# Attention scores in four PSUM banks: one exponential of 2048 columns a round, or two of 1024

## The chip, the cores and the metric

The kernel runs on one core of one Trainium2 chip. The core has a matrix engine (PE, with its weight loads shown apart as PEld), a vector engine (DVE), an activation engine (ACT), a general-purpose engine (POOL) and a queue that issues transfers (SP). Each works through its own queue in order and waits on semaphores for the others. The matrix engine writes its results to PSUM, which this kernel uses as eight banks, each 512 float32 wide on 128 partitions; everything else here lives in SBUF or in main memory. The metric is the time of one execution on the device, in microseconds (us); the median of several is taken.

## The reference

The program is two layers of a transformer-like network on an input of 8 images, 128 channels and 32 x 32 = 1024 tokens, float32 throughout. The change touches only the first mixing step, an attention with 8 heads of 16 channels. Of the reference, what matters is this:

```python
q = (xp @ wq.T).reshape(b, h, w, n, d)
k = (xp @ wk.T).reshape(b, h, w, n, d)
v = (xp @ wv.T).reshape(b, h, w, n, d)
weights = jnp.einsum('bhwnd,bxynd->bnhwxy', q, k) * scale
weights = jax.nn.softmax(weights, axis=-1)
attn = jnp.einsum('bnhwxy,bxynd->bhwnd', weights, v)
```

The softmax runs over `y`, the 32 columns of one key row, and not over all 1024 keys: every query has 32 softmaxes for each head, one for each key row, and the results of all rows are added up. After the attention come a spectral convolution over the tokens, a convolution with learned offsets and a mixture of experts; they are not touched.

## The kernel before, in words

**Stages.** A first stage of some 28 us loads the weights and checks a bound on the scores, by which the kernel chooses `attention_bounded` (line 500). This attention runs over all 8 images. After it comes the spectral stage, mixed with the second layer, to the end of the program.

**Tiling of the attention.** An image has two head groups (`HG` = 2) of four heads (`NH` = 4), and four blocks of 256 queries (`QU` = 256). One head group of one query block is a *unit*: 8 units for an image, 64 in all. A unit takes four *rounds*, `r` = 0 to 3, one for each pair of key tiles of 128 keys; there are 256 rounds. In a round, `scores` (line 601) takes a tile `s` of 128 x 4 x 2 x 256 float32: head `j` has PSUM bank `j`, and within a bank the first 256 columns are key tile `c` = 0 and the second 256 are key tile `c` = 1. Eight matmuls fill it. In the program each float32 matmul is two instructions, so the profile counts 16. Then one activation takes the exponential of all 2048 columns into `e` in SBUF. The pool of `s` has one buffer (line 520), so the next round's matmuls wait until this exponential has read the banks.

**What follows a round's exponential.** `add_tiles` (line 620) adds the two key tiles on POOL. `sums` (line 626) contracts the sums over key columns on PE, all four `r` of a unit together, 32 instructions. `reciprocals` (line 635) inverts them on DVE, `spread_out` (line 639) spreads the result over the partitions on PE (tile `rb`, two banks), `divide` (line 649) multiplies `e` by it on DVE, `values` (line 655) multiplies with the values on PE, 16 instructions for an `r`. `take` and `results` hand a query block on. The projections of the next image (`keys`, `queries`, `key_values`, lines 560 to 599) and its normalisation are strewn between, each with a matmul group on PE and a copy on ACT. PSUM is full: four banks for `s`, two for `rb`, one for `av`, and one (`small_bank`, line 532) that `z` and all the small steps take in turn.

**What sets the order.** No planner: each step is entered in a list by `at(round, order, step)` (line 693), the list is sorted by round and then by order, and the steps are issued so (lines 758 to 760); every engine's queue has its instructions in this order. In a round, the order is `scores` (0), `add_tiles` (1), `values` (2), `spread_out` (2.5), `divide` (3), `sums` (4), `reciprocals` and `take` (5), pieces of other work (5.5, 6), and a half step of `values` (6.5). For a unit that starts in round `t0`, the sums come in `t0+5`, the spreading in `t0+6`, the divisions in `t0+6` to `t0+9`, the values in `t0+8` to `t0+11`. So the rounds have four kinds, by their number modulo four, and in the steady state PE's queue holds in each:

| kind | round mod 4 | PE's queue, in order |
|---|---|---|
| A | 0 | scores, values (16), pieces, values (8) |
| B | 1 | scores, values (8), sums (32) |
| C | 2 | scores, values (16), spread_out (8) |
| D | 3 | scores, values (16), pieces |

Of the kernel before, what the change touches and what calls it, by code (L numbers as in the profile page):

```python
# [11 lines left out]
F32 = mybir.dt.float32  # L12
I32 = mybir.dt.int32
AF = mybir.ActivationFunctionType
# [4 lines left out]
P = 128  # L19
# [6 lines left out]
HD = C // HEADS  # L26
# [37 lines left out]
def layer_norm_pieces(nc, pool, src, dst, eps):  # L64

    t = {}

    def stats(i):  # L70
        if i == 0:
            for name, shape in (
                ("st", [P, NT, 6]), ("mv", [P, NT, 2]), ("v", [P, NT]), ("y", [P, NT]),
                ("w", [P, NT]), ("nm", [P, NT]),
            ):
                t[name] = pool.tile(shape, F32, tag=f"lp_{name}", name=f"lp_{name}")
        nc.vector.bn_stats(t["st"][:, i, :], src()[:, i, :])
        nc.vector.bn_aggr(t["mv"][:, i, :], t["st"][:, i, :])

    def inverse(n):  # L80

        v, y, w, mv = t["v"], t["y"], t["w"], t["mv"]
        bits = [i.bitcast(I32) for i in (y, v)]
        ops = [
            lambda: nc.gpsimd.tensor_scalar(v, mv[:, :, 1], eps, None, ALU.add),
            lambda: nc.gpsimd.tensor_scalar(bits[0], bits[1], -0.5, 0x5F3759DF, ALU.mult, ALU.add),
            lambda: nc.gpsimd.tensor_scalar(v, v, -0.5, None, ALU.mult),
        ]
        ops += 3 * [
            lambda: nc.gpsimd.tensor_mul(w, y, y),  # L90
            lambda: nc.gpsimd.tensor_mul(w, w, v),
            lambda: nc.gpsimd.tensor_scalar(w, w, 1.5, None, ALU.add),
            lambda: nc.gpsimd.tensor_mul(y, y, w),
        ]
        ops += [
            lambda: nc.gpsimd.tensor_mul(t["nm"], mv[:, :, 0], y),
            lambda: nc.gpsimd.tensor_scalar(t["nm"], t["nm"], -1.0, None, ALU.mult),
        ]
        for op in ops[2 * n : 2 * n + 2]:
            op()  # L100

    def norm(i):
        nc.scalar.activation(
            dst()[:, i, :], src()[:, i, :], AF.Identity, bias=t["nm"][:, i : i + 1],
            scale=t["y"][:, i : i + 1],
        )

    return (
        [partial(stats, i) for i in range(NT)] + [partial(inverse, n) for n in range(9)]
        + [partial(norm, i) for i in range(NT)]  # L110
    )
# [288 lines left out]
class BoundedAttention:  # L400
# [3 lines left out]
    NH = 4  # L404
# [95 lines left out]
def attention_bounded(ctx, tc, ident, x, x1d, given, weigh, begin_group):  # L500
# [8 lines left out]
    nc = tc.nc  # L509
    NH, HG = given.NH, given.HG  # L510
    QU = 256
# [7 lines left out]
    ep = ctx.enter_context(tc.tile_pool(name="a_e", bufs=11))  # L519
    sp = ctx.enter_context(tc.tile_pool(name="a_s", bufs=1, space=PSUM))  # L520
    rp = ctx.enter_context(tc.tile_pool(name="a_r", bufs=1, space=PSUM))

    VB = 2 * (P + HD)
# [72 lines left out]
            pv.rearrange("p (a j d) -> p a j d", j=NH, d=HD),  # L598
        )

    def scores(img, un, r):

        qc, hg = un["at"]
        s = sp.tile([P, NH, 2, QU], F32, tag="s", name="s")
        q = img["q"][:, hg].rearrange("p a t -> p (a t)")
        for c in range(2):
            for j in range(NH):
                rows = slice(32 * j, 32 * j + 32)
                nc.tensor.matmul(  # L609
                    s[:, j, c, :], img["k"][rows, hg, 2 * r + c, :],  # L610
                    q[rows, qc * QU : (qc + 1) * QU], start=True, stop=True,
                )
        e = ep.tile([P, NH, 2, QU], F32, tag="e", name="e")
        nc.scalar.activation(  # L614
            e.rearrange("p j c q -> p (j c q)"), s.rearrange("p j c q -> p (j c q)"), AF.Exp,
            scale=float(HD) ** -0.5,
        )
        un["e", r] = e

    def add_tiles(un, r):  # L620
        t = sb.tile([P, NH, QU], F32, tag="t", name="t", bufs=6)
# [71 lines left out]
    def at(round_no, order, do, *args):  # L693
        work.append((round_no, order, len(work), do, args))

    def spread_rounds(pieces, rounds):
        for piece, round_no in zip(pieces, rounds):
            at(round_no, 6, piece)

    for b in range(B):  # L700
        img = {}
        first = 4 * UNITS * b
        project = [
            (keys, img, 0, 0), (keys, img, 0, 1), (queries, img, 0, 0),
            (keys, img, 1, 0), (keys, img, 1, 1), (queries, img, 1, 0),
            (key_values, b, img, 0), (key_values, b, img, 1),
            (queries, img, 0, 1), (queries, img, 1, 1),
        ]
        if b == 0:
            turn = {"tokens": (0, 0)}  # L710
            project_at = (-1, -1, -1, 0, 1, 2, 3, 4, 7, 11)
        else:
            project_at = [first + n for n in (-13, -12, -9, -5, -4, -1, 3, 4, 7, 11)]
            turn = {"channels": (first - 20, first - 17)}
            if b == 1:
                turn.update(load=0, tokens=(2, 3))
                norm_at = (3, 3, 4, 4, 5, 5, 6, 6) + (6, 7, 7, 8, 8, 8, 9, 9, 9) + (
                    10, 10, 10, 11, 13, 13, 14, 14)
            else:
                turn.update(load=first - 42, tokens=(first - 38, first - 34))  # L720
                norm_at = [first - n for n in (
                    37, 36, 35, 34, 33, 32, 32, 31, *range(31, 22, -1), 22, 22, 22, 21, 19, 19, 18, 18
                )]
        if b:
            at(turn["load"], 6, load, b)
            spread_rounds(
                layer_norm_pieces(nc, sb, lambda i=img: i["xt"], lambda: given.ht, 1e-6), norm_at
            )
            for par in range(2):
                at(turn["channels"][par], 5.5, channels, par)  # L730
        for par in range(2):
            at(turn["tokens"][par], 5.5, tokens, img, par)
        for n, (step, when) in enumerate(zip(project, project_at)):
            if b == 0 and n < 3:
                at(-1, 6, weigh[n])
            at(when, 6, *step)
        for qc in range(QC):
            qrt = {}
            for hg in range(HG):
                un = {"at": (qc, hg)}  # L740
                t0 = first + 4 * (HG * qc + hg)
                for r in range(4):
                    at(t0 + r, 0, scores, img, un, r)
                    at(t0 + r, 1, add_tiles, un, r)
                    at(t0 + 5, 4, sums, un, r)
                    at(t0 + 6 + r, 3, divide, un, r)
                at(t0 + 8, 2, values, img, un, 0, (0, 1), qrt)
                at(t0 + 8, 6.5, values, img, un, 1, (0,), qrt)
                at(t0 + 9, 2, values, img, un, 1, (1,), qrt)
                at(t0 + 10, 2, values, img, un, 2, (0, 1), qrt)  # L750
                at(t0 + 11, 2, values, img, un, 3, (0, 1), qrt)
                at(t0 + 5, 5, reciprocals, un)
                at(t0 + 6, 2.5, spread_out, un)
            at(t0 + 11, 5, take, qrt)
            at(t0 + 12, 6, results, b, img, qc, qrt)
# [938 lines left out]
def metaformer_kernel(  # L1694
# [27 lines left out]
    with tc.If(bounded > P - 1) as branch:  # L1722
        with ExitStack() as part:
            attention_bounded(part, tc, ident, x, x1d, given, weigh, begin.pieces)
# [63 lines left out]
```

## Time and profile before

| | us |
|---|---|
| median of 3 runs (2657.89 to 2663.11) | 2662.8 |
| the profiled execution, its own time | 2658.17 |
| its span, first to last instruction | 2656.4 |
| the attention: first score matmul to the start of the last one | 27.9 to 885.1 |
| of this, per round (256 rounds) | 3.35 |
| the window from 100 to 740 us: PE busy | 637.11 of 640 |
| the same window: DVE, ACT, POOL busy | 527.54, 438.45, 492.38 |

The profile is of one execution. Its page gives busy times of the engines and the costliest groups of instructions; further views answer on one window, one tile, the waits, or the order of time. A line such as `t<-e` names what is written and what is read; in square brackets stands how long the engine sat idle before, and what released it. The window from 100 to 740 us lies wholly inside the attention and holds 192 of its rounds. The ends of matmuls are modelled, so that PE counts as busy while its pipeline empties.

### The profile page before, as it was taken

The page shows a single profiled execution, that of the slowest core. Times are in us where ns is not written, and L with a number is a line of the kernel's source. Part 1 is how long each engine was busy: PE and PEld are TensorE (multiplying, and loading weights), DVE is VectorE, ACT ScalarE, POOL GpSimd, SP SyncE. Part 2 cuts the span into 40 slices and gives each one's busy share as a digit, 9 for nine tenths or more (in the row PEclk, how much of TensorE's full clock was granted, in tenths as well). Part 3 has the DMA queues.
Part 4 walks back from the last instruction along what each step waited for, and adds up shares of the span by engine and source line. Part 5 has one row for each costly group of instructions (what it writes and reads, how often), then busy time and mean ns, then how long its engine had stood idle before and what let it go on. Part 6 is the DMA issues. An engine that isn't in the chain of part 4 may idle for free. (4 is left out here: it accounts for less than half of the span.)

```text
span 2656.4 us, 47332 instructions
## 1 busy us (share of the span) xinstructions
PE 2500.7 (94%) x18768; PEld 1750.2 (66%) x18768; DVE 1852.6 (70%) x2800; ACT 1064.2 (40%) x1982; POOL 1449.2 (55%) x1535
## 2 busy tenths in 40 slices
PE   6999999999999789999999999999999999999924
PEld 3555555555555468878778778778778778778612
DVE  3788888888888545549749748658658658658656
ACT  4676766667766311124214214224224224224222
POOL 4777777877778555446246237237337337236230
PEclk9999999999999999999999999999999999999966
DMA  1000000000000154465365266266356357256160
GB/s 30 2 18 2 18 17 2 18 2 18 10 18 18 57 165 157 145 191 176 99 189 180 91 182 192 87 183 188 98 168 201 100 154 215 92 144 213 48 182 20
DMA packets 214531, 271.29 MB, mean 102 GB/s; under 512 B 20948, under 2 KB 147092, under 8 KB 214304
## 3 DMA queue, kind: packets, MB, share of 16 engines
q1 hardware_dynamic: 197504, 212.61, 26.6%
q0 software_dynamic: 16800, 55.59, 6.3%
q8 instruction: 150, 2.46, 0.4%
q14 instruction: 77, 0.63, 0.1%
HBM read 200.22 MB, written 67.92 MB: 101 GB/s over the span
## 5 line engine op out<-in xcount | busy, mean ns | idle before, releaser
L623 POOL TENSOR_TENSOR t<-e 128x1024 f32<-128x1024 f32 x256 | 608.2, 2376 | 198.9 <-ACT e L614 198.7
L651 DVE TENSOR_TENSOR e<-e,rb 128x2048 f32<-128x2048 f32 x256 | 570.8, 2277 | 84.5 <-PE rb L644 84.5
L614 ACT ACTIVATE e<-s 128x2048 f32<-128x2048 f32 x256 | 481.1, 1879 | 253.0 <-PE s L609 250.5
L1557 POOL TENSOR_TENSOR part<-us,part 128x256 f32<-128x256 f32 x256 | 191.0, 746 | 705.6 <-ACT part L1556 698.7
L1509 PE MATMUL po<-us,mf 128*128 128x128 f32 (+2 forms) x2048 | 528.1, 381 | 5.8 <-DVE mf L1441 5.8
L1555 ACT COPY us<-p_x 128x256 f32<-128x256 f32 x256 | 95.2, 372 | 753.8 <-PE p_x L1544 740.6
L1562 DVE TENSOR_TENSOR part<-p_y,part 128x512 f32<-128x512 f32 x256 | 175.3, 685 | 289.3 <-PE p_y L1544 200.2
L1509 PEld LDWEIGHTS po<-us,mf 128*128 128x128 f32 x2048 | 308.8, 191 | 37.8 <-DVE mf L1441 6.2
L609 PE MATMUL s<-q,k 32*128 32x256 f32 x4096 | 295.9, 403 | 15.2 <-ACT e L614 14.4
L661 PE MATMUL av<-e,vt 128*32 128x256 f32 x4096 | 288.2, 389 | 4.0 <-DVE e L651 2.7
L1572 DVE TENSOR_TENSOR us<-p_z,part 128x512 f32<-128x512 f32 x256 | 174.8, 683 | 159.3 <-PE p_z L1544 159.2
L609 PEld LDWEIGHTS s<-q,k 32*128 32x128 f32 x4096 | 186.4, 185 | 137.9 <-ACT e L614 116.6
L1544 PEld LDWEIGHTS p_z<-diff,gap 128*128 128x128 f32 x1024 | 191.9, 189 | 125.3 <-issue 87.5
L1544 PE MATMUL p_z<-diff,gap 128*128 128x256 f32 x1024 | 263.4, 379 | 3.1 <-DVE base L907 3.1
L661 PEld LDWEIGHTS av<-e,vt 128*32 128x32 f32 x4096 | 101.4, 109 | 141.6 <-issue 84.7
L1091 POOL DMA_INDIRECT g<-tab,here x168 | 165.9, 988 | 43.2 <-issue 37.0
L1109 ACT ACTIVATE g<-g,w 128x128 f32<-128x128 f32 x448 | 140.1, 393 | 74.2 <-DMA g<-tab,here 73.2
L1299 POOL TENSOR_TENSOR diff<-teto 128x516 f32<-128x516 f32 x127 | 165.0, 1299 | 2.2 <-DMA teto<-in_phi_o 1.4
L1117 DVE TENSOR_REDUCE x<-g 128x128 f32<-128x1536 f32 x56 | 158.7, 2834 | 5.0
L637 DVE RECIPROCAL r<-z 128x256 f32<-128x256 f32 x64 | 112.5, 1757 | 71.3 <-PE z L630 71.1
L1544 PE MATMUL p_y<-diff,gap 128*128 128x256 f32 x512 | 152.9, 380 | 2.4 <-POOL diff L1299 2.3
L1544 PE MATMUL p_x<-teto,ht 128*128 128x256 f32 x512 | 131.4, 379 | 0.0
(268 smaller groups left out, 3708.9 us busy)
## 6 DMA issues: line engine op xcount, KB each, us to landing
mf<-mfd SPq DMA_DIRECT2D x112, 512.0 KB
tab<-gs SPq DMA_DIRECT2D x192, 256.0 KB
teto<-in_phi_o SPq DMA_DIRECT2D x127, 256.5 KB
teto<-in_phi_e SPq DMA_DIRECT2D x127, 256.0 KB
mfd<-mf SPq DMA_DIRECT2D x16, 512.0 KB
xc<-in_x SPq DMA_DIRECT2D x8, 512.0 KB
x1d<-xt SPq DMA_DIRECT2D x8, 512.0 KB
m_room<-in_M_plus SPq DMA_DIRECT2D x16, 256.0 KB
```

Source lines behind the costliest of these rows:

```text
L609: nc.tensor.matmul(s[:, j, c, :], img["k"][rows, hg, 2 * r + c, :], q[rows, qc * QU : (qc + 1) * QU], start=True, stop=True,)
L614: nc.scalar.activation(e.rearrange("p j c q -> p (j c q)"), s.rearrange("p j c q -> p (j c q)"), AF.Exp, scale=float(HD) ** -0.5,)
L623: nc.gpsimd.tensor_add(t, e[:, :, 0, :], e[:, :, 1, :])
L651: nc.vector.tensor_tensor(e, e, un["rb"].unsqueeze(2).to_broadcast([P, NH, 2, QU]), ALU.mult)
L661: nc.tensor.matmul(qrt["av"][32 * j : 32 * j + 32, 0:QU], img["v"][:, 2 * r + c, P * hg + 32 * j : P * hg + 32 * j + 32], un["e", r][:, j, ...
L1091: nc.gpsimd.indirect_dma_start(out=tiles[-1][:, tap].rearrange("p k c -> p (k c)"), out_offset=None, in_=rows[tap], in_offset=bass.Indirec ...
L1299: lambda: nc.gpsimd.tensor_sub(blocks[:, :, 0:2], pair, one),
L1509: self.nc.tensor.matmul(out, lhsT, rhs, start=bank not in img["opened"], stop=last, skip_group_check=True)
L1544: nc.tensor.matmul(out, weights, moving, start=start, stop=stop, skip_group_check=True)
L1557: nc.gpsimd.tensor_add(part[:, 0], mine[:, :, 0:P], part[:, 1])
L1562: nc.vector.tensor_tensor(part[:, 2:4], y[:, 0].unsqueeze(1).to_broadcast([C, 2, 2, P]), part[:, 0:2], ALU.add)
L1572: nc.vector.tensor_tensor(result(2, 4), z, part[:, 2:4], ALU.add)
```

## The change

The tile `s` is taken once, ahead of the loops, instead of once a round. `scores` does one key tile at a time: four matmuls (eight instructions) into the half of every bank that belongs to key tile `c`, and an exponential of 4 x 256 = 1024 columns of that half alone. The first half stays at order 0. The second is entered at order 2.7, behind `values` and `spread_out` of the round, and `add_tiles`, which needs both, goes from order 1 to 2.8. So PE's queue in a round reads: scores of key tile 0, values, spread_out, scores of key tile 1, sums, pieces, values.

```diff
+    s = sp.tile([P, given.NH, 2, QU], F32, name="s")
...
-    def scores(img, un, r):
+    def scores(img, un, r, c):
 
         qc, hg = un["at"]
-        s = sp.tile([P, NH, 2, QU], F32, tag="s", name="s")
         q = img["q"][:, hg].rearrange("p a t -> p (a t)")
-        for c in range(2):
-            for j in range(NH):
-                rows = slice(32 * j, 32 * j + 32)
-                nc.tensor.matmul(
-                    s[:, j, c, :], img["k"][rows, hg, 2 * r + c, :],
-                    q[rows, qc * QU : (qc + 1) * QU], start=True, stop=True,
-                )
-        e = ep.tile([P, NH, 2, QU], F32, tag="e", name="e")
-        nc.scalar.activation(
-            e.rearrange("p j c q -> p (j c q)"), s.rearrange("p j c q -> p (j c q)"), AF.Exp,
-            scale=float(HD) ** -0.5,
-        )
-        un["e", r] = e
+        for j in range(NH):
+            rows = slice(32 * j, 32 * j + 32)
+            nc.tensor.matmul(
+                s[:, j, c, :], img["k"][rows, hg, 2 * r + c, :],
+                q[rows, qc * QU : (qc + 1) * QU], start=True, stop=True,
+            )
+        if c == 0:
+            un["e", r] = ep.tile([P, NH, 2, QU], F32, tag="e", name="e")
+        nc.scalar.activation(un["e", r][:, :, c, :], s[:, :, c, :], AF.Exp, scale=float(HD) ** -0.5)
...
-                    at(t0 + r, 0, scores, img, un, r)
-                    at(t0 + r, 1, add_tiles, un, r)
+                    at(t0 + r, 0, scores, img, un, r, 0)
+                    at(t0 + r, 2.7, scores, img, un, r, 1)
+                    at(t0 + r, 2.8, add_tiles, un, r)
```

## The prediction

> **What bounds the kernel now.** I read the page first, for the shares of the engines over the whole span and for the groups that the change touches.
>
> ```profile
> PE 2500.7 (94%) x18768; PEld 1750.2 (66%) x18768; DVE 1852.6 (70%) x2800; ACT 1064.2 (40%) x1982; POOL 1449.2 (55%) x1535
> ...
> L614 ACT ACTIVATE e<-s 128x2048 f32<-128x2048 f32 x256 | 481.1, 1879 | 253.0 <-PE s L609 250.5
> ...
> L609 PE MATMUL s<-q,k 32*128 32x256 f32 x4096 | 295.9, 403 | 15.2 <-ACT e L614 14.4
> ```
>
> ACT waits 250.5 us for the score matmuls; PE itself waits only 14.4 us for the exponentials. Next the busy times and the waits of a window inside the attention (100 to 740 us, 192 rounds).
>
> ```profile
> 100.00:740.00 640.00, 637.11 (x8454) 347.17 (x8452) 527.54 (x336) 438.45 (x373) 492.38 (x318) 1.00 0.03 11
> ```
>
> ```profile
> ACT e L614 <- PE s L609: 185.6, 184, 1.5
> ...
> PEld s L609 <- ACT e L614: 78.8, 159, 0.8
> PEld av L661 <- issue: 63.8, 180, 0.8
> ```
>
> PE is the bound: 637.11 of 640 us, at a granted clock of 1.00. But the weight loads of the scores waited 159 times for an exponential, so a second limit lies just under it. The order of time shows both, over one unit.
>
> ```profile
> 404.23 1.15 PE L609 MATMUL s<-q,k 32*128 32x256 f32 x16
> ...
> 405.30 1.07 PE L661 MATMUL av<-e,vt 128*32 128x256 f32 x16
> 405.51 1.88 ACT L614 ACTIVATE e<-s 128x2048 f32<-128x2048 f32 x1 [0.76 <-PE s L609]
> ...
> 406.30 1.13 PE L644 MATMUL rb<-r,spread 64*128 64x256 f32 x8
> ...
> 407.44 1.15 PE L609 MATMUL s<-q,k 32*128 32x256 f32 x16
> ...
> 410.64 1.15 PE L609 MATMUL s<-q,k 32*128 32x256 f32 x16 [0.46 <-ACT e L614]
> ...
> 413.93 1.15 PE L609 MATMUL s<-q,k 32*128 32x256 f32 x16
> ...
> 415.46 1.91 PE L630 MATMUL z<-t,group 128*32 128x256 f32 x32
> ...
> 417.30 1.15 PE L609 MATMUL s<-q,k 32*128 32x256 f32 x16
> 417.44 1.76 DVE L637 RECIPROCAL r<-z 128x256 f32<-128x256 f32 x1 [1.00 <-PE z L630]
> ```
>
> From start to start a round takes 3.21 (C), 3.20 (D), 3.29 (A) and 3.37 (B), 13.07 a unit; 64 units are 836 of the 857 us that the attention lasts, the other 21 being rounds with more pieces. The loop scores, exponential, scores takes 1.28 (404.23 to 405.51; 1.25 to 1.28 elsewhere, I use 1.26) + 1.88 + 0.05 (end at 407.39, next start 407.44) = 3.19. It just fits into a round, while PE does values, sums and spreading under it.
>
> [...] Here every bank holds both key tiles. The trace has no case of a half written while the other is read; it has the reverse order, in the first stage:
>
> ```profile
> 5.25 1.91 PE L438 MATMUL p_x<-ident,xc 128*128 128x128 f32 x8
> ...
> 6.35 0.50 DVE L441 BATCH_NORM_STATS2 f_st<-p_x 128x6 f32<-128x128 f32 x2 [6.35 <-PE p_x L438]
> ```
>
> Four of these eight transposes fill a bank, and DVE first reads only the first one's 128 columns. At 0.42 each (the tile's minimum and maximum, starts 5.25 to some 6.74, so 0.213 apart), the first ends at 5.67 and the fourth at 6.31. DVE starts at 6.35: this program orders by bank. [...] no PE line overtakes a score group. [...] the window shows 1.00, so I keep full clock.
>
> **The change part by part.** *The halves.* By the bank order, key tile 1's matmuls wait for key tile 0's exponential, and the next round's key tile 0 for key tile 1's. The one loop of a round becomes two in a row. A hop is:
> - matmuls to exponential: 1.26 less half the 16 instructions. They come (1.15 - 0.37) / 15 = 0.052 apart (0.37 is the shortest duration of one), so 1.26 - 8 x 0.052 = 0.84. At 1.07 / 16 = 0.067 apart it would be 0.73; bound above 0.95, if halving saves less.
> - the exponential of 1024 columns, not in the trace. Copies of 512 columns take 0.59, the exponential of 2048 takes 1.88: 0.84 ns a column, so 0.59 + 0.43 = 1.02. [...] I take 1.02.
> - exponential to matmuls: 0.05.
>
> Hop H = 1.91, between 1.80 and 2.04. A round cannot be under 2H = 3.82, against 3.19.
>
> *What fits under the two hops.* A half group keeps PE 1.07 - 0.42 = 0.65 (start of the scores to start of what follows, less eight instructions), leaving about 1.26 of a hop.
> - A: values 1.00 (405.30 to 406.30) under the first hop; values of 8 instructions (some 0.57 to the next scores) and results (0.64) under the second. 3.82.
> - D: values under the first, a piece of 1.13 under the second. 3.82.
> - B: 0.45 of values under the first. Behind the second half come the sums, 1.84 (415.46 to 417.30), more than the hop holds: H + 0.65 + 1.84 = 4.40.
> - C: before, the reciprocal started 2.06 after the sums' first matmul (402.38 to 404.44), took 1.76, and was done at 406.20, just as the values ended; the spreading was not delayed. Now the sums start at 2.56 of B, the reciprocal ends at 6.38, that is 1.98 of C, whose values end at 1.65. The spreading starts at 2.08 and takes 1.12; the second half, queued behind it, starts at 3.20 instead of 1.91. 3.20 + H = 5.11.
>
> The unit: 3.82 + 4.40 + 5.11 + 3.82 = 17.15 against 13.07; 64 x 4.08 = +261 us. The extra pieces cost 21 before; now a projection in A overhangs by 0.44 three times an image, and three normalisations in a row on ACT (3 x 0.44 after an exponential, with 0.88 to spare) once by 0.44: some 14 for 8 images, so -7. Net +254.
>
> *Activations.* 256 more, 2 x 1.02 - 1.88 = 0.16 more busy time a round, 41 us of ACT, counted in H and in no sum again. Without the waits, ACT's idle time (201 of 640) would hide it.
> *add_tiles moved* behind the second exponential: nothing. POOL has 2.38 to do in a round of 4.29. The sums need it two rounds later; if POOL were late, the sums would stretch B. It passes no transfer but the indirect ones at order 7, still behind it. No other transfer moves and SP's queue stays.
> *Static tile:* same four banks, nothing else freed or taken.
> *divide* on DVE: four of 2.22 and a reciprocal fit in 17.15; nothing.
>
> The profiled execution took 2658.17 (1.8 around its span); plus 254 is 2912. The median stands 4.6 above this execution: **2917**. With H at its ends the unit is 6H + 5.69, 16.49 or 17.93: 2875 to 2967.
>
> **Rivals.**
> 1. *Only the chain:* the overhangs of B and C do not show, because sums and spreading find room. 8H = 15.28, 64 x 2.21 = +141: 2804. For it: DVE, with some 11 us of work a unit, has slack, so a slightly earlier reciprocal is served at once. Against: the order puts the sums behind the second half and the spreading ahead of it.
> 2. *Order by bytes, half groups keep their switch cost.* No wait between the halves. Each round pays 2 x 0.65 - 1.07 = 0.23, and C still exposes the reciprocal by 2.08 - 1.65 = 0.43: 1.35 a unit, +86: 2749. For it: the 63.8 us of weight loads idle after scores without a releaser show that a change of tiling costs even where nothing is awaited. Against: the bank order at 6.35.
> 3. *Faster: order by bytes, and the switch cost was the wait.* Then a half group is 8 x 0.0535 = 0.43, and two save 0.21 a round, 0.84 a unit; the spreading is exposed by 2.08 - 1.43 = 0.65. -0.19 a unit, -12: 2651; if the reciprocal hides too, 2609. It decides in one place: whether the first weight load of key tile 1 waits for the exponential of key tile 0.
>
> **How the numbers follow.** The mechanism computed: 0.74. Rival 1: 0.10, rival 2: 0.08, rival 3: 0.05, and 0.03 for worse [...]. The time is the likeliest one's, 2917, its own range 2875 to 2967. Down to 2780 rival 1 comes in, and rivals 2 and 3 are left out with the 0.03: 2780 to 2970. A difference under 0.2% (5 us) can't be told from none in this kernel. Faster 0.04, same 0.01 (rival 3's spread), slower 0.95.
>
> **What would show it.** In the changed profile: 512 activations of 1024 columns at about 1.02; the weight loads of `s` waiting for `e` in nearly every half; PE busy near 75% of the attention, which ends near 1140; no PE line `s` starting before the preceding exponential's end; B and C the long rounds, with `rb` waiting for `r` by some 0.4. If key tile 1's matmuls start while key tile 0's exponential runs, the prediction is wrong at its first step. If rounds B and C are as short as A and D, rival 1 holds.

## The result, and the profile after

The changed kernel takes 2902.36 us (median of 4 runs, 2900.73 to 2909.2), the kernel before 2661.43 us (median of 4, 2657.89 to 2663.11). The ratio is 1.0914, 95% interval 1.0902 to 1.0927: slower by 9%. The prediction was 2917 us, its range 2780 to 2970; the loss was forecast as 254 us and came out as 241.

All of it lies in the attention. The score matmuls now run from 27.8 to 1128.7 us, 1100.9 us against 857.2 before: 243.7 us more. The span grew by the same (2900.2 - 2656.4 = 243.8). What comes after the attention takes as long as before.

The profile page, busy times and costliest groups, shows twice as many exponentials, of half the width, and waits of PE's that were not there:

```profile
PE 2595.9 (90%) x18768; PEld 1721.6 (59%) x18768; DVE 1861.7 (64%) x2800; ACT 1105.0 (38%) x2238; POOL 1446.4 (50%) x1535
...
L615 ACT ACTIVATE e<-s 128x1024 f32<-128x1024 f32 x512 | 524.5, 1024 | 470.6 <-PE s L609 464.5
...
L609 PE MATMUL s<-q,k 32*128 32x256 f32 x4096 | 369.3, 430 | 152.1 <-ACT e L615 142.5
L609 PEld LDWEIGHTS s<-q,k 32*128 32x128 f32 x4096 | 161.4, 184 | 390.5 <-ACT e L615 336.9
```

The matmuls of the scores now wait 142.5 us for exponentials (14.4 before), their weight loads 336.9 us (116.6 before, in the view of tile `s`). ACT in turn waits 464.5 us for PE. Each waits for the other.

The window from 100 to 740 us: first the busy times (columns as before: the window, then PE, PEld, DVE, ACT, POOL, the granted clock, the transfers), then two lines of the waits.

```profile
100.00:740.00 640.00, 549.33 (x6604) 252.93 (x6604) 415.70 (x270) 364.59 (x439) 382.47 (x242) 1.00 0.02 8
```

```profile
DVE r L634 <- PE z L627: 181.6, 38, 5.5
...
PE s L609 <- ACT e L615: 75.4, 144, 1.2
```

PE, busy 637.11 of these 640 us before, is busy 549.33, and no engine has taken its place: the bound is a chain of waits. DVE's wait for the sums (181.6 us, 46.6 before) is for the most part slack, since DVE is busy for 415.70 of the 640 us; what the late reciprocal costs PE shows only in round C, below.

From here on a *hop* is the way from a half's score matmuls through its exponential to the next half's score matmuls. The order of time, rounds B (from 504.30), C (from 508.69), D (from 513.67) and A (from 517.44), to the next B:

```profile
504.30 0.71 PE L609 MATMUL s<-q,k 32*128 32x256 f32 x8
...
505.11 1.02 ACT L615 ACTIVATE e<-s 128x1024 f32<-128x1024 f32 x1 [0.39 <-PE s L609]
...
506.18 0.71 PE L609 MATMUL s<-q,k 32*128 32x256 f32 x8 [0.60 <-ACT e L615]
...
506.83 1.93 PE L627 MATMUL z<-t,group 128*32 128x256 f32 x32
...
508.69 0.71 PE L609 MATMUL s<-q,k 32*128 32x256 f32 x8
508.91 1.76 DVE L634 RECIPROCAL r<-z 128x256 f32<-128x256 f32 x1 [5.08 <-PE z L627]
...
510.72 1.14 PE L641 MATMUL rb<-r,spread 64*128 64x256 f32 x8 [0.31 <-DVE r L634]
...
511.79 0.71 PE L609 MATMUL s<-q,k 32*128 32x256 f32 x8
...
512.59 1.02 ACT L615 ACTIVATE e<-s 128x1024 f32<-128x1024 f32 x1 [2.02 <-PE s L609]
...
513.67 0.71 PE L609 MATMUL s<-q,k 32*128 32x256 f32 x8 [1.17 <-ACT e L615]
...
515.56 0.71 PE L609 MATMUL s<-q,k 32*128 32x256 f32 x8 [0.17 <-ACT e L615]
...
517.44 0.71 PE L609 MATMUL s<-q,k 32*128 32x256 f32 x8 [0.58 <-ACT e L615]
...
521.21 0.71 PE L609 MATMUL s<-q,k 32*128 32x256 f32 x8
```

Follow one hop: scores at 504.30, their exponential at 505.11, done at 506.13, the second half's scores at 506.18, 1.88 us on. In none of these rounds does a half start before the preceding exponential is done. Start to start, B takes 4.39, C 4.98, D 3.77 and A 3.77: 16.91 a unit, against 13.07. In C one sees what lies under the long wait: the reciprocal ends at 510.67, the spreading starts at 510.72, the second half only at 511.79, and ACT has been idle for 2.02 us.

### The profile page after: what moved, and what is told of

The parts are those of the page before. It is cut to its first block, busy times and chain, and to the rows that moved or that the text cites. A ratio compares the mean times of both kernels' runs of the same rounds, so it can differ in the third digit from the quotient of the medians.

```text
span 2900.2 us, 47608 instructions
## 1 busy us (share of the span) xinstructions
PE 2595.9 (90%) x18768; PEld 1721.6 (59%) x18768; DVE 1861.7 (64%) x2800; ACT 1105.0 (38%) x2238; POOL 1446.4 (50%) x1535
## 5 line engine op out<-in xcount | busy, mean ns | idle before, releaser
L615 ACT ACTIVATE e<-s 128x1024 f32<-128x1024 f32 x512 | 524.5, 1024 | 470.6 <-PE s L609 464.5
L609 PE MATMUL s<-q,k 32*128 32x256 f32 x4096 | 369.3, 430 | 152.1 <-ACT e L615 142.5
L609 PEld LDWEIGHTS s<-q,k 32*128 32x128 f32 x4096 | 161.4, 184 | 390.5 <-ACT e L615 336.9
L1542 PE MATMUL p_z<-teto,ht 128*128 128x256 f32 x512 | 132.1, 380 | 0.0
```

The costliest lines, as they stand in the source:

```text
L609: nc.tensor.matmul(s[:, j, c, :], img["k"][rows, hg, 2 * r + c, :], q[rows, qc * QU : (qc + 1) * QU], start=True, stop=True,)
L615: nc.scalar.activation(un["e", r][:, :, c, :], s[:, :, c, :], AF.Exp, scale=float(HD) ** -0.5)
L1542: nc.tensor.matmul(out, weights, moving, start=start, stop=stop, skip_group_check=True)
```

## The experiments

The theory was: halves that share banks are ordered, so two hops in a row replace one loop (3.77 us a round instead of 3.19), and in rounds B and C PE's other work hangs over. Rivals: the short exponentials themselves cost; the overhangs don't matter; the score tile is ordered as a whole and not by bank.

**Two exponentials, nothing else.** The kernel before, with only the activation cut in two:

```diff
-        nc.scalar.activation(
-            e.rearrange("p j c q -> p (j c q)"), s.rearrange("p j c q -> p (j c q)"), AF.Exp,
-            scale=float(HD) ** -0.5,
-        )
+        for c in range(2):
+            nc.scalar.activation(e[:, :, c, :], s[:, :, c, :], AF.Exp, scale=float(HD) ** -0.5)
```

> The kernel before, with its exponential of 2048 columns cut into two of 1024, one per key tile, right behind each other; all score matmuls stay together at order 0. Theory (the loss comes from the second half's matmuls queueing for the first half's exponential): only the extra fixed cost of one activation is added to the loop, 1.26 + 1.94 + 0.05 = 3.25 us against 3.19, which lengthens rounds C and D by some 0.05 each: about +6 us, 2667 us (2660 to 2690). Rival (the two short exponentials themselves, their strided reading or ACT's load, are what costs): most of the 241 us show here, 2740 us or more.

Measured: 2665.81 us, ratio 1.0021 (1.0011 to 1.0031), +4.8 us by the medians. In its order of time the two run back to back in 1.94 us. The short exponentials are not what costs; their extra fixed time is worth about 5 of the 241 us.

**The second half ahead of the spreading.**

```diff
-                    at(t0 + r, 2.7, scores, img, un, r, 1)
+                    at(t0 + r, 2.4, scores, img, un, r, 1)
```

> The changed kernel with the second half at order 2.4, ahead of the spreading (2.5), instead of 2.7. Theory (in round C the spreading, late with the reciprocal, holds up the second half): C falls from 4.98 to 3.77 us, 64 x 1.21 = 77 us less: 2825 us. Rival (the lateness only moves on, into the divisions and values behind it, or C is long for another reason): 2880 us or more.

Measured: 2836.75 us (ratio to the kernel before 1.0659, 1.0642 to 1.0677), 65.6 us under the changed kernel. The order of time, one round C and the scores that open the next round:

```profile
517.85 0.71 PE L609 MATMUL s<-q,k 32*128 32x256 f32 x8
518.01 1.76 DVE L634 RECIPROCAL r<-z 128x256 f32<-128x256 f32 x1 [3.55 <-PE z L627]
...
519.73 0.71 PE L609 MATMUL s<-q,k 32*128 32x256 f32 x8 [0.17 <-ACT e L615]
...
520.37 1.13 PE L641 MATMUL rb<-r,spread 64*128 64x256 f32 x8
...
521.61 0.71 PE L609 MATMUL s<-q,k 32*128 32x256 f32 x8
```

C takes 3.76 us, as expected, with the spreading under the second hop. PE follows the order of the list in both runs: spreading at 510.72 and second half at 511.79 there, second half at 519.73 and spreading at 520.37 here. The gain stays 11 us short of 77: two rounds C of an image also hold the transposes of its tokens, which now hang over behind the spreading (in the next run such a round, from 517.94 to 522.26, takes 4.32), 13 such rounds in all, 13 x 0.56 = 7 us. The other 4 us I did not trace. So the late spreading in C cost about a quarter of the loss.

**And the sums split.**

```diff
-                    at(t0 + 5, 4, sums, un, r)
+                    at(t0 + 5, 2.3 if r < 2 else 4, sums, un, r)
```

> As the run with the second half ahead of the spreading, and besides the sums of r = 0 and 1 at order 2.3, ahead of round B's second half, those of r = 2 and 3 behind it as they were. Theory (round B is long because 1.84 us of sums do not fit under one hop): B falls from 4.39 to about 3.89, 64 x 0.5 = 32 us less: 2793 us. What is then left over the kernel before, about 132 us, is the doubled chain alone, two hops of 1.88 in every round. Rival (the sums are held by POOL or DVE, not by their place): no change against the run before it, 2825 us.

Measured: 2807.7 us (1.0557, 1.0539 to 1.0574), 29 us less than the run before it. Round B, from the order of time:

```profile
513.98 0.71 PE L609 MATMUL s<-q,k 32*128 32x256 f32 x8
...
515.08 1.05 PE L627 MATMUL z<-t,group 128*32 128x256 f32 x16
...
516.06 0.71 PE L609 MATMUL s<-q,k 32*128 32x256 f32 x8
...
516.71 1.07 PE L627 MATMUL z<-t,group 128*32 128x256 f32 x16
...
517.94 0.71 PE L609 MATMUL s<-q,k 32*128 32x256 f32 x8 [0.17 <-ACT e L615]
```

B takes 3.96 us instead of 4.39, 0.43 x 64 = 28 us. Reordering alone has now taken away 94 of the changed kernel's 241 us: work that its order left without cover in B and C. Of the 147 us that are left, two hops in every round come to some 129, an estimate from 64 x (4 x 3.77 - 13.07); 12 are what B still has over two hops (0.19 x 64), and the 6 that remain are about what the rounds with the transposes add.

**Nothing under the first hop.**

```diff
-                    at(t0 + r, 2.7, scores, img, un, r, 1)
+                    at(t0 + r, 0.1, scores, img, un, r, 1)
```

> The changed kernel with the second half at order 0.1, right behind the first, so that nothing else lies in PE's queue under the first exponential. Theory: PE then idles through the first hop, 1.24 us of it in each round, and all of its other work has to come after: A 4.42, B 4.82, C 4.6, D 3.53 and 1.74 of pieces, 19.1 a unit: about 3030 us (2990 to 3070). So the order 2.7 hides work worth some 130 us. Rival (PE's work under the first hop is hidden in any order, by the loop of the next round): no change, 2902 us.

Measured: 3014.7 us (1.1335, 1.1315 to 1.1355), 112 us above the changed kernel. PE's matmuls wait 302.0 us for exponentials over the attention, in place of 142.5. Putting the values between the halves was worth this much; it hid PE's work, not the chain.

**Halves without a common bank.** To see whether the bank makes the second half wait, I cut by heads: heads 0 and 1 lie in banks 0 and 1, heads 2 and 3 in banks 2 and 3.

```diff
-        for j in range(NH):
-            rows = slice(32 * j, 32 * j + 32)
-            nc.tensor.matmul(
-                s[:, j, c, :], img["k"][rows, hg, 2 * r + c, :],
+        for half in range(2):
+            for j in range(2 * c, 2 * c + 2):
+                rows = slice(32 * j, 32 * j + 32)
+                nc.tensor.matmul(
+                    s[:, j, half, :], img["k"][rows, hg, 2 * r + half, :],
...
-        nc.scalar.activation(un["e", r][:, :, c, :], s[:, :, c, :], AF.Exp, scale=float(HD) ** -0.5)
+        js = slice(2 * c, 2 * c + 2)
+        nc.scalar.activation(un["e", r][:, js], s[:, js], AF.Exp, scale=float(HD) ** -0.5)
```

> The changed kernel with the halves cut by heads instead of key tiles: heads 0 and 1 (banks 0 and 1) at order 0, heads 2 and 3 (banks 2 and 3) at order 2.7. No bank is shared between the halves; [...] a half costs PE about 1.11 us (as the eight spreading instructions do) instead of 0.65. Theory (the wait is by bank): the second half no longer waits for the first half's exponential; in round B its matmuls start while that exponential still runs, the idle time of the score weight loads before an exponential falls from 337 us to under 100, and the time is set by PE's work alone, A 4.11, B 4.51, C 4.33, D 3.22 and 1.74 of pieces: 17.9 a unit, about 2955 us (2850 to 2970). Rival (the tile s, taken once, is ordered as a whole): the waits stay, a hop is about 2.37, a unit 19.5 or more: 3000 to 3100 us.

Measured: 3372.58 us (1.2606, 1.251 to 1.2701), above what either theory gave. The order of time from the end of a round C into round D, then the window of 100 to 740 us:

```profile
620.52 1.02 ACT L617 ACTIVATE e<-s 128x1024 f32<-128x1024 f32 x1 [3.54 <-PE s L610]
...
621.60 1.13 PE L610 MATMUL s<-q,k 32*128 32x256 f32 x8 [0.48 <-ACT e L617]
...
622.78 1.02 ACT L617 ACTIVATE e<-s 128x1024 f32<-128x1024 f32 x1 [0.76 <-PE s L610]
...
623.85 0.73 PEld L610 LDWEIGHTS s<-q,k 32*128 32x128 f32 x8 [0.60 <-ACT e L617]
```

```profile
100.00:740.00 640.00, 599.68 (x4594) 306.62 (x4590) 285.10 (x178) 258.60 (x312) 266.97 (x180) 0.77 0.02 6
```

Two things. The next round's first half, in banks 0 and 1, starts at 621.60, 0.06 after the exponential of banks 2 and 3 ends (621.54); the second half, in banks 2 and 3, starts at 623.85, 0.05 after the exponential of banks 0 and 1 (623.80). They share no bank and wait for each other: it is not the bank that orders them in this program. And PE's granted clock is 0.77, where every other run has 1.00 in this window, so that the time of this run can't be read for the waits.

**The same, with a tile for each half.** The only edit against the run above:

```diff
-    s = sp.tile([P, given.NH, 2, QU], F32, name="s")
+    pairs = [sp.tile([P, 2, 2, QU], F32, name=f"s{n}") for n in range(2)]
...
-                    s[:, j, half, :], img["k"][rows, hg, 2 * r + half, :],
+                    pairs[c][:, j - 2 * c, half, :], img["k"][rows, hg, 2 * r + half, :],
...
-        nc.scalar.activation(un["e", r][:, js], s[:, js], AF.Exp, scale=float(HD) ** -0.5)
+        nc.scalar.activation(un["e", r][:, js], pairs[c], AF.Exp, scale=float(HD) ** -0.5)
```

> As the run with the halves cut by heads (banks 0 and 1, banks 2 and 3), where the second half still waited for the first half's exponential although it shares no bank with it; now each half is a tile of its own, two banks each. Everything else is the same. Theory (the program orders accesses to one tile as a whole, coarser than by bank): the waits between the halves go, in round B the second half's matmuls start while the first exponential runs, the score weight loads' idle time before an exponential falls from 316 us to under 100, and PE's work alone is left, 17.9 us a unit at full clock: some 2955 us, up to 3200 if PE's clock stays as low as in that run (0.72 to 0.83 over the attention). Rival (the order was by bank after all and something else held the second half, PE's own queue or its lowered clock): the waits stay and the time stays near 3370 us.

Measured: 2870.33 us (1.0778, 1.0761 to 1.0794). The order of time in a round B, then the same window:

```profile
507.18 1.02 ACT L617 ACTIVATE e<-s 128x1024 f32<-128x1024 f32 x1 [0.99 <-PE s L610]
...
507.63 1.13 PE L610 MATMUL s<-q,k 32*128 32x256 f32 x8
...
508.69 1.93 PE L629 MATMUL z<-t,group 128*32 128x256 f32 x32
```

```profile
100.00:740.00 640.00, 636.77 (x6656) 349.62 (x6650) 414.82 (x270) 361.68 (x440) 384.27 (x249) 1.00 0.02 8
```

The second half's matmuls start 0.45 us into the first exponential. Score matmuls wait 1.6 us for exponentials over the attention, their weight loads 56.5. PE is the bound again (636.77 of 640), its clock is 1.00, and the time is above the kernel before because a half with two of the four heads costs PE 1.06 us from start to start (507.63 to 508.69; its eight instructions take 1.13, those of a half with all four heads 0.71), so that two of them take 1.05 more than the whole group's 1.07; over 256 rounds that is up to 269 us, against 207 by which the run is slower. So this program orders the accesses to the score tile as a whole. PE's own work came to 1070.8 / 64 = 16.7 us a unit, not 17.9: my sum of it was 7% too high.

Not every tile is ordered so. In the kernel before, the scores that open an image read one part of its query tile `q`, in SBUF, while ACT writes another part of the same tile, by a copy that stands ahead of these scores in the list:

```profile
783.40 1.15 PE L609 MATMUL s<-q,k 32*128 32x256 f32 x16
...
783.49 0.60 ACT L569 COPY q<-pq 128x512 f32<-128x512 f32 x1
```

Why the program orders `s` as a whole and `q` by its parts, no run here tests.

**Two exponentials by banks, matmuls together.** With that, a version that might win: all score matmuls at order 0 as before, the exponential cut between banks 1 and 2. First in one tile, which is taken once ahead of the loops as in the changed kernel; against the first run above the edit is:

```diff
-        for c in range(2):
-            nc.scalar.activation(e[:, :, c, :], s[:, :, c, :], AF.Exp, scale=float(HD) ** -0.5)
+        for h in range(2):
+            js = slice(2 * h, 2 * h + 2)
+            nc.scalar.activation(e[:, js], s[:, js], AF.Exp, scale=float(HD) ** -0.5)
```

> The kernel before with two exponentials of 1024 columns cut by banks (heads 0 and 1, heads 2 and 3), all score matmuls together at order 0, and the tile s taken once. The first exponential can start when twelve of sixteen instructions are through, and the next round's first four matmuls wait for it alone. Theory (PE's own work bounds the kernel before, and the waits are by bank): the loop shortens from 3.19 to about 2.94 us, which only rounds D without pieces can use: 2650 to 2662 us, 0 to 11 us faster than before. Rival (the loop through the exponential bounds the kernel before): 0.2 us a round, 50 us faster, about 2610 us. If the tile is ordered as a whole: 2667 us, as with two exponentials by key tile.

Measured: 2665.55 us (1.0022, 1.0012 to 1.0031), close to the 2667 that was given for a tile ordered as a whole, and the same as with the cut by key tiles. The score matmuls wait 14.8 us for exponentials over the attention, 15.0 with the cut by key tiles. Taking the tile once, which the changed kernel does too, costs nothing that shows here. Then with a tile for each pair of heads:

```diff
+    pairs = [sp.tile([P, 2, 2, QU], F32, name=f"s{n}") for n in range(2)]
...
-                    s[:, j, c, :], img["k"][rows, hg, 2 * r + c, :],
+                    pairs[j // 2][:, j % 2, c, :], img["k"][rows, hg, 2 * r + c, :],
...
-            nc.scalar.activation(e[:, js], s[:, js], AF.Exp, scale=float(HD) ** -0.5)
+            nc.scalar.activation(e[:, js], pairs[h], AF.Exp, scale=float(HD) ** -0.5)
```

> As the run with two exponentials cut by banks and all score matmuls together at order 0, but with a tile of two banks for each pair of heads. If the tile is what is ordered, the first exponential now starts after twelve of sixteen instructions and the next round's first four matmuls wait for it alone; the loop falls from 3.25 to about 2.94 us. PE's own work bounds the kernel before, so only rounds D without pieces can use it: 2650 to 2662 us, against 2659 before. If the loop through the exponential were the bound of the kernel before, 0.2 us a round, some 50 us, would be won: about 2610 us. If the order is not by tile: 2666 us, as in the run with one tile.

Measured: 2659.66 us, ratio 0.9986 (0.9979 to 0.9992): 3.5 us under the kernel before. The interval lies below 1, but this is less than the 5 us that the prediction took as the least difference one can tell here. The order of time in a round D, then the window of 100 to 740 us:

```profile
410.39 1.94 ACT L616 ACTIVATE e<-s 128x1024 f32<-128x1024 f32 x2 [0.45 <-PE s L609]
...
411.89 1.63 PE L609 MATMUL s<-q,k 32*128 32x256 f32 x16
```

```profile
100.00:740.00 640.00, 640.00 (x8484) 352.78 (x8480) 529.13 (x337) 450.80 (x565) 493.79 (x319) 1.00 0.03 11
```

The next round's scores start at 411.89, before the second exponential ends at 412.33; over the attention score matmuls wait 2.7 us for exponentials, 14.4 in the kernel before. PE is busy for all of the 640 us. The loop through the exponential has been loosened, and there were no more than these few us behind it: the kernel before was bound by PE's work, as the prediction read it.

What was not tried: two tiles that share a bank, unordered with each other. So whether the bank alone would have forced the wait of the changed kernel stays open here; the tile, which holds both halves, is enough for it.

## Why the prediction was right, point by point

*PE bounds the kernel before, the loop just under it.* Right; the version with two tiles shows it from the other side.

*One loop becomes two hops.* Right in what happens, and near in size: a hop is 0.81 + 1.02 + 0.05 = 1.88 us, predicted 0.84 + 1.02 + 0.05 = 1.91. Rounds A and D: 3.77, predicted 3.82.

*The exponential of 1024 columns.* 1.024 us mean, predicted 1.02 from the copies' slope. The prediction's upper end of a hop, 2.04, is 0.02 above what its parts from the trace give (0.95, itself an estimate, + 1.02 + 0.05); that 0.02 was not shown.

*B.* 4.39, predicted 4.40. *C.* 4.98, predicted 5.11. The reciprocal ended 1.98 us into C, as computed (that it agrees to the hundredth is luck: the sums started 2.53 us into B instead of 2.56, the reciprocal 2.08 after them instead of 2.06); the spreading started at 2.03 (2.08), and from it to the second half it was 1.07, not 1.12.

*The sum.* 64 x (16.91 - 13.07) = 246 against 261 predicted: A and D, 0.05 each, B, 0.01, and C, 0.13, make the difference. The odd pieces add 1100.9 - 64 x 16.91 = 18.7 us, where I had put 14: -2 instead of -7. Together 243.7, predicted 254.

*Why the halves are ordered.* Here a step failed, though the number stood. "This program orders by bank" was read from first-stage transposes that fill one bank of one tile, and that line can't tell the bank from the tile. Halves in banks of their own waited for each other inside one tile too (96.4 us of score matmuls waiting for exponentials), and stopped waiting as two tiles (1.6 us). That a shared bank forces an order was the author's assumption; no run here shows it. Had the change cut by heads in one tile, the bank argument would have forecast free halves and missed.

*Two edits costed at nothing* held: no matmul of the sums waited for POOL's addition, and the values waited 4.0 us in all for DVE's divisions. *PE's busy share* did not: I said near 75% and the window shows 86%. I had left out that two half groups cost PE 0.23 us a round more than one whole group (0.65 each, 506.18 to 506.83, against 1.07, 404.23 to 405.30 before), though rival 2 had that number. It accounts for 5 of the 11 points (4 x 0.23 of 16.91); the other 6 I did not trace. *Nearly every half* was too much as well: the weight loads waited for an exponential 379 times in 512 halves.

*The rivals.* The first, the chain alone, is not what the changed kernel does, but its price was near (141, measured 147 once B and C were put in order). That is luck in part: with the measured hops it would have been 129, and the other 18 us are overhangs that stayed. The second and third, order by bytes, are excluded by the order of time. The cost of a change of tiling, on which both turn, is in the order of time before: eight instructions of the values take 0.57 up to the scores (413.36 to 413.93), and 0.46 up to the sums, which are tiled 128*32 as they are (415.00 to 415.46). *Clock:* 1.00, as assumed, with PE busy for 549.33 of the 640 us; that it would hold with such gaps was not shown beforehand.

## What to carry to other kernels

Splitting a producer and consumer into halves buys overlap only if nothing orders the halves among themselves; inside one PSUM tile, this program ordered them, even in separate banks, and then every half costs a full round trip through the other engine, here 1.88 us twice instead of 3.19 once. Before splitting, count the fixed part of a trip (0.86 us of 1.88 was not exponential) and look whether the engine that waits is already full: if it is, shortening the loop wins next to nothing (3.5 us here), while doubling it loses at once. In a hand-written order, a stretched chain also uncovers whatever was placed to fit under the old one: here at least 94 of 241 us.

## What was not expected of the hardware

In the run with head-wise halves in one tile, PE's granted clock was 0.77 over 100 to 740 us, and eight score instructions took 2.08 us in some stretches (at 150.23, say) and 1.13 in others. The same instructions in two tiles ran at 1.00. More idle time alone is not the reason: with the halves in a row PE was busy for 480.98 of the 640 us, the longest wait of a score matmul for an exponential was 1.3 us, and the clock was 1.00 too; in the run at 0.77 PE was busy for 599.68, and the longest such wait was 1.1 us. The cause stays open.
